# A four-layer graph network on one core: layer 2's own rows moved into the tile of the listed columns, the dense bank copied by ScalarE

## The chip, the core and the metric

The kernel runs on one core of a Trainium2 chip. The metric is device time in microseconds (us) of one execution. Its instructions go to five engines that run side by side, each in its own order: TensorE (matrix products, "PE" in the profile; "PEld" is its weight loads), VectorE (DVE), ScalarE (ACT), GpSimd (POOL) and SyncE (SP), which here only issues DMA transfers. "SPq" marks an issue of a DMA on SyncE's queue. The order on each engine is set when the program is built, by a planner that works with its own estimates of durations; it is not the order of the lines.

## The reference, cut to what matters

Four graph layers over 2708 nodes with 512 features, each of the form `x = x + layer(relu(layernorm(x)), adj)`. The change is in layer 2, a two-step graph convolution, and in the indices that layer 3 shares with it:

```python
def _L2_gnn_ref(x, adj, W1, b1, W3, b3, Wf, bf):
    h = jax.nn.relu(adj @ (x @ W1) + b1)
    h = jax.nn.relu(adj @ (h @ W3) + b3)
    return jnp.tanh(h @ Wf + bf)

def _L3_gnn_ref(input_features, adj, W, b):
    A = (adj != 0).astype(input_features.dtype)
    hidden = input_features @ W + b
    deg = jnp.sum(A, axis=0)
    return A @ hidden / deg[:, None]

h = jnp.maximum(_layernorm(x, axis=-1), 0.0)
x = x + _L2_gnn_ref(h, adj, L2_gnn_W1, L2_gnn_b1, L2_gnn_W3, L2_gnn_b3, L2_gnn_Wf, L2_gnn_bf)
```

`adj` is sparse, and the denser towards the first nodes, with a full diagonal.

## The kernel before

The 2708 rows are worked on in 22 row tiles of 128 (the last, tile 21, has 20 rows). For a row tile `m` the product `adj @ g` has three parts.

- **Dense part**: the first `WHOLE[m]` column tiles (6 for the first tiles, 3 or 4 later) are multiplied in full. Each piece of the matrix (`raw`, up to three column tiles, loaded on SP at L1013) is split into a high, a low and a combined part (ScalarE L1068, VectorE L1069 and L1070), and so is `g`. The products (L1081) collect in two banks of TensorE's accumulator memory: `agg` (called `main` in the function) and `aggs` (`mixed`).
- **Listed part**: of the columns behind, only those with a nonzero are taken. Their numbers were found in layer 0 and stand in `idx_g`, in up to `CHUNKS[m]` chunks of 128 (10 for tile 1, then 9, 8, 7 and on down to 5). The listed columns of the matrix stand in DRAM (`listed[m]`, `lst` in the profile) and are loaded by `load_listed` (SP, L1023) into a tile `ac`, of which there are two buffers. The matching rows of `g` are gathered from DRAM by GpSimd (L1030), one indirect DMA for a chunk, into eight buffers `gg`. The products (L1084) go to `aggs`.
- **Own rows**: for tiles 6 to 20 (`alone(m)`) the diagonal isn't in the lists. The rows of `g` with the tile's own numbers are loaded (SP, L1107) into `u`, multiplied by the diagonal `diag_c` and the bias is added (VectorE, L1108).

`aggregated` then sums the banks: `u = agg * (1 - 2^-12) + bias`, `u = aggs * 2^-12 + u` (both VectorE, L1115; for own rows `bias` is the `u` of L1108). `agg` and `aggs` have two buffers each. `relu_parts` transposes `u` on TensorE (`pt`, L970) and splits it into `v_hi` (ScalarE, L975), `v_lo` and `v_s` (VectorE, L976 and L979), and `project3` multiplies by weights in three parts into the banks `main` and `mixed` (L995).

This happens in two passes over the row tiles. The **first pass** reads `g1d` and writes `g2d` (the products by W3). It also marks the nonzeros for layer 3: ScalarE writes the signs of `ac` and `raw` to `nz` (L1048), stored at L1100. The **second pass** reads `g2d`, and behind the first projection (`main<-wa`, by Wf) a chain runs for each tile: `sum_banks` writes `z` (ScalarE L956, VectorE L957), the bias is added (L1391), tanh (ScalarE L1392, with a load of its table), the residual is added (L1400), layernorm follows (L189 to L199, with another table load), and after a second transpose the second projection (`main<-wb`) gives layer 3's `hidden`. It is stored to `hid` (L1408) and, from tile 3 on, to `hidr` (L1411). The tile `z` carries the name `u` too, so the sums of the banks and `z` share two buffers of that name, which they take in turn. Layer 3 then gathers rows of `hidr` with a second set of indices, `idx_h`, which is `idx_g` less 384 (L1382, in program order behind `aggregated`, for tiles 4 to 20); tile 21 uses `idx_g` and `hid`.

The pool `ap` holds `raw` (three buffers), `ac` (two), `nz` (three) and the split parts; the pool `wp` holds `u`, `v_*` and `go` (two buffers each). Layer 3 uses the name `ac` for its masks (L1305).

The lines of the step around the change:

```python
u = wp.tile([P, D], FP, name="u")
if alone(m):
    nc.sync.dma_start(out=u, in_=gd[span(m)])
    nc.vector.scalar_tensor_tensor(
        u, u, diag_c[:, m : m + 1], bias, op0=ALU.mult, op1=ALU.add
    )
    bias = u
main, mixed = aggregate(m, parts, shifted, gd, marked)
```

Of the kernel before, what the change touches and what calls it, by code (L numbers as in the profile page):

```python
# [9 lines left out]
FP = mybir.dt.float32  # L10
# [34 lines left out]
def kernel(  # L45
# [36 lines left out]
    NB = (N + BLK - 1) // BLK  # L82
    UNIT = 4
    assert N % UNIT == 0
    NCH = 8 * ((max(CHUNKS) + 7) // 8)
    NCA = max(CHUNKS)
    NCL = max(CHUNKS[LEAD:])

    def rows(t):
        return min(P, N - t * P)  # L90
# [60 lines left out]
    flag = const.tile([P, 1], I32, name="flag")  # L151


    idx_g = const.tile([P, NT, NCH], U32, name="idx_g")

    rdeg = const.tile([P, NT], FP, name="rdeg")
    diag_c, self_w = (const.tile([P, NT], FP, name=name) for name in ("diag_c", "self_w"))
# [81 lines left out]
    with tc.tile_pool(name="l0_slab", bufs=2) as slabs, tc.tile_pool(  # L239
# [177 lines left out]
        def search(m):  # L417

            first = dense_of(m) * P
            num = N - first  # L420
            ranks = ranks_of.pop(m)

            end = wp.tile([P, 1], FP, name="end")
            nc.vector.tensor_scalar_add(end, ranks[:, num - 1 : num], 1.0)
            nc.vector.tensor_copy(ranks[:, num : num + 1], end)
            want = wp.tile([P, NCH], FP, name="want")
            nc.vector.tensor_scalar(want, places, end, None, op0=ALU.min)
            for c0 in range(0, CHUNKS[m], 8):
                c = slice(c0, c0 + 8)
                at = wp.tile([P, 8], U32, name="found")  # L430
                nc.vector.max_index(at, want[:, c], ranks)
                nc.vector.tensor_scalar(
                    idx_g[:, m, c],
                    at,
                    float(N - first),
                    float(first),
                    op0=ALU.min,
                    op1=ALU.add,
                )
                node = wp.tile([P, 8], FP, name="node")  # L440
                nc.vector.tensor_scalar(
                    node,
                    at,
                    float(N - 1 - first),
                    float(N // UNIT),
                    op0=ALU.min,
                    op1=ALU.mult,
                )
                nc.vector.tensor_scalar_add(
                    idx_a[:, m, c], node, float((first * N + m * P) // UNIT)  # L450
                )
            nc.vector.tensor_scalar(
                bad[:, BAD_MANY + m : BAD_MANY + m + 1],
                end,
                float(CHUNKS[m] * P + 1),
                None,
                op0=ALU.is_gt,
            )
# [189 lines left out]
        def gather_rows(m):  # L648

            gs = []  # L650
            for c in range(CHUNKS[m]):
                g = hp.tile([P, D], FP, name=f"h{DENSE + gather_slot[0] % NGG}")
                gather_slot[0] += 1
                nc.gpsimd.indirect_dma_start(  # L654
                    out=g,
                    out_offset=None,
                    in_=h0d[:, :],
                    in_offset=bass.IndirectOffsetOnAxis(ap=idx_g[:, m, c : c + 1], axis=0),
                )
                gs.append(g)  # L660
            gathers[m] = gathers[m], gs
# [280 lines left out]
    order_2 = order_m[:1] + order_m[HEAD:] + order_m[1:HEAD]  # L942
    x3_last = dram.tile([P, D], FP, name="x3_last")

    idx_h = gp.tile([P, NT, NCA], U32, name="idx_h")
    NMARK = DENSE + NCA
    gather_slot = [0]

# [70 lines left out]
        return raw[:k, : len(ts), :n], k  # L1019

    def load_listed(m):
        ac = ap.tile([P, NCA, P], FP, name="ac")[:, : CHUNKS[m], : rows(m)]
        nc.sync.dma_start(out=ac, in_=listed[m])  # L1023
        return ac

    def gather(m, gd, gs=None, index=idx_g):

        gs = gs or [gathered() for _ in range(CHUNKS[m])]
        for c in range(CHUNKS[m]):
            nc.gpsimd.indirect_dma_start(  # L1030
                out=gs[c],
                out_offset=None,
                in_=gd[:, :],
                in_offset=bass.IndirectOffsetOnAxis(ap=index[:, m, c : c + 1], axis=0),
            )
        return gs

    def aggregate(m, parts, shifted, gd, marked):


        n = rows(m)
        whole, num = dense_of(m), CHUNKS[m]
        if marked:
            nz = ap.tile([P, NMARK, P], U8, name="nz", bufs=3)

            def mark(i, a):
                k, ts = a.shape[:2]
                nc.scalar.activation(nz[:k, i : i + ts, :n], a, AF.Sign)  # L1048
        main = ps_a.tile([P, D], FP, name="agg") if dense_of(m) else None
        mixed = ps_a.tile([P, D], FP, name="aggs")  # L1050
        chunks = []
        if num:
            ac = load_listed(m)
            chunks = [(ac[:, c, :], g) for c, g in enumerate(gather(m, gd))]
            if marked:
                mark(whole, ac)
        for ts in ([t for t in ts if t < whole] for ts in dense):
            if not ts:
                continue
            gs = [parts(t) for t in ts]  # L1060
            raw, k = load_piece(m, ts)
            hi, lo, s = (
                ap.tile([P, PIECE, P], FR, name=f"a_{part}") for part in ("hi", "lo", "s")
            )
            d = (slice(0, k), slice(0, len(ts)), slice(0, n))
            if marked:
                mark(ts[0], raw)
            nc.scalar.activation(hi[d], raw, AF.Copy, scale=UP)  # L1068
            nc.vector.tensor_tensor(lo[d], raw, hi[d].bitcast(FP), ALU.subtract)  # L1069
            nc.vector.scalar_tensor_tensor(  # L1070
                s[d], lo[d].bitcast(FP), SHIFT, hi[d].bitcast(FP), op0=ALU.mult, op1=ALU.add
            )
            for i, t in enumerate(ts):
                ghi, glo, gs_ = gs[i]
                first, last = t == 0, t == whole - 1
                for acc, a, b, st, sp in (
                    (main, hi, ghi, first, False),
                    (main, lo, glo, False, last),
                    (mixed, s, gs_, first, False),
                ):  # L1080
                    nc.tensor.matmul(acc[:n], a[:k, i, :n], b[:k], start=st, stop=sp)  # L1081
        if chunks:
            for c, (a, g) in enumerate(chunks):
                nc.tensor.matmul(  # L1084
                    mixed[:n],
                    a,
                    g,
                    start=(c == 0 and not dense_of(m)),
                    stop=(c == len(chunks) - 1),
                )  # L1090
        else:
            for ts in others:
                gs = [shifted(t) for t in ts]
                raw, k = load_piece(m, ts)
                for i, t in enumerate(ts):
                    nc.tensor.matmul(  # L1096
                        mixed[:n], raw[:, i, :], gs[i][:k], start=False, stop=(t == NT - 1)
                    )
        if marked:
            nc.sync.dma_start(out=nonzero[m], in_=nz[:, : whole + num, :n])  # L1100
        return main, mixed

    def aggregated(m, parts, shifted, gd, bias, marked=False):
        n = rows(m)
        u = wp.tile([P, D], FP, name="u")
        if alone(m):
            nc.sync.dma_start(out=u, in_=gd[span(m)])  # L1107
            nc.vector.scalar_tensor_tensor(  # L1108
                u, u, diag_c[:, m : m + 1], bias, op0=ALU.mult, op1=ALU.add
            )  # L1110
            bias = u
        main, mixed = aggregate(m, parts, shifted, gd, marked)
        if dense_of(m):
            for bank, scale in ((main, 1.0 - EPS12), (mixed, EPS12)):
                nc.vector.scalar_tensor_tensor(  # L1115
                    u[:n], bank[:n], scale, bias[:n], op0=ALU.mult, op1=ALU.add
                )
                bias = u
        else:
            nc.vector.scalar_tensor_tensor(  # L1120
                u[:n], mixed[:n], EPS12, bias[:n], op0=ALU.mult, op1=ALU.add
            )
        return relu_parts(u, n)
# [138 lines left out]
    def gather_h(m):  # L1262
# [1 line left out]
        whole, num = dense_of(m), CHUNKS[m]  # L1264
        nz = marks[m] = ap.tile([P, NMARK, P], U8, name="nz", bufs=3)
        nc.sync.dma_start(out=nz[:, : whole + num, : rows(m)], in_=nonzero[m])
        gd, index = (hidr, idx_h) if whole else (hid, idx_g)
        listed_h[m] = gather(m, gd, [next(places_h) for _ in range(num)], index)

    def bank_h(m):  # L1270
        if m not in banks:
# [30 lines left out]
    def listed_products(m):  # L1302
        n = rows(m)
        whole, num = dense_of(m), CHUNKS[m]
        mask = ap.tile([P, NCA, P], FR, name="ac")[:, :num, :n]  # L1305
        nc.scalar.copy(mask, marks[m][:, whole : whole + num, :n])
        for c, g in enumerate(listed_h.pop(m)):
            high = part_room()
# [67 lines left out]
    for m in order_2:  # L1376
# [3 lines left out]
            w = split_w(wsetb, wr, "wb")  # L1380
        if dense_of(m) and m not in FULL:
            nc.vector.tensor_scalar_add(  # L1382
                idx_h[:, m, : CHUNKS[m]], idx_g[:, m, : CHUNKS[m]], float(-HEAD * P)
            )
        if m == order_2[-1]:
            for k in order_3[:FIRST]:
# [498 lines left out]
```

## Time and profile before

| what | value |
|---|---|
| three runs, median (lowest to highest) | 1461.38 us (1460.47 to 1461.90) |
| the profiled execution | 1461.3 us |
| its span | 1459.5 us |
| mean granted TensorE clock | 0.929 of full |
| busy: TensorE, VectorE, ScalarE, GpSimd | 1240.7, 954.0, 675.8, 660.6 us |

The page's second part shows the span in 40 equal slices of 36.5 us; each digit is a busy share in tenths, and PEclk is the clock granted to TensorE in tenths:

```profile
PE   4898897889787559989899989899988888967997
DVE  4677996897998568743344356356655666656776
ACT  5865465576344446522222223244443444435563
PEclk9989998989898869999999999999999999978999
```

Layer 2's sums of the banks (L1115) start between 597.5 and 1284.2 us: the first pass stores its last g2d at 908.9 (L1192), the first gather of the second pass starts at 912.1, and the loads of own rows go out from 703.5 to 884.5 and from 986.1 to 1246.0 (L1107). Layer 3 follows. A group in the page's list of groups reads: line, engine, operation, tile written <- tiles read, number of instructions, then busy time and mean duration, then the idle time of the engine just before them with what ended it:

```profile
L1084 PE MATMUL aggs<-gg,ac 128*128 128x512 f32 (+1 forms) x520 | 237.0, 598 | 5.2 <-DMA gg<-g1d,idx_g 5.2
L1108 DVE SCALAR_TENSOR_TENSOR u<-u,diag_c,bias 128x512 f32<-128x512 f32 x30 | 22.6, 752 | 60.5 <-DMA u<-g1d 46.9
```

The first line is the listed products of both passes: two instructions for a chunk, 598 ns each (they overlap). The second is the step of the own rows, 15 tiles in each pass: 752 ns each, and VectorE stood 60.5 us before them in all, 46.9 of it for the first pass's loads. In the lists of waits a line reads: engine, tile and line that waited <- what it waited for: us in total, times, longest. In the lists of instructions: start, duration, engine, line, operation, and in brackets the idle time of the engine before it.

### The profile page before, as it was taken

The numbers are of one execution on the slowest core, as the hardware profiler recorded it, in microseconds if no ns is written. First come the engines' busy times: TensorE is split into PE (matmuls) and PEld (weight loads), VectorE is DVE, ScalarE is ACT, GpSimd is POOL, SyncE is SP. The second block draws the span as 40 slices with busy tenths as digits, with TensorE's granted clock in tenths as the row PEclk, the third lists the DMA queues.
The fourth block names the chain that finished last, engine by engine and source line by source line (L and its number), as shares of the span: only waits on it lengthen the run. The fifth ranks groups of instructions, "written<-read, shape, count | busy, mean of one in ns | idle before, by whom it ended". The sixth has DMA issues, their size and how long they took to land. (4 is left out here: it accounts for less than half of the span.)

```text
span 1459.5 us, 15175 instructions
## 1 busy us (share of the span) xinstructions
PE 1240.7 (85%) x4223; PEld 725.9 (50%) x4223; DVE 954.0 (65%) x2043; ACT 675.8 (46%) x1056; POOL 660.6 (45%) x674
## 2 busy tenths in 40 slices
PE   4898897889787559989899989899988888967997
PEld 2333333334333146746455556466645555545775
DVE  4677996897998568743344356356655666656776
ACT  5865465576344446522222223244443444435563
POOL 1245567656662431055545441444524232355773
PEclk9989998989898869999999999999999999978999
DMA  9988997999886488367868876856746455558895
GB/s 350 339 253 281 330 297 241 315 291 308 260 304 218 130 290 281 112 213 256 261 210 260 272 245 211 268 189 211 216 140 194 144 162 161 172 177 304 278 300 164
DMA packets 187750, 350.68 MB, mean 240 GB/s; under 512 B 22818, under 2 KB 96496, under 8 KB 183925
## 3 DMA queue, kind: packets, MB, share of 16 engines
q1 hardware_dynamic: 140057, 202.48, 42.2%
q0 software_dynamic: 46032, 145.05, 31.5%
q10 hardware_dynamic: 1568, 2.10, 0.4%
q8 instruction: 35, 0.57, 0.2%
q14 instruction: 58, 0.48, 0.1%
HBM read 285.96 MB, written 63.58 MB: 239 GB/s over the span
## 5 line engine op out<-in xcount | busy, mean ns | idle before, releaser
L1030 POOL DMA_INDIRECT gg<-g2d,idx_g x130 | 133.8, 1029 | 244.4 <-PE aggs L1084 200.0
L1084 PE MATMUL aggs<-gg,ac 128*128 128x512 f32 (+1 forms) x520 | 237.0, 598 | 5.2 <-DMA gg<-g1d,idx_g 5.2
L1030 POOL DMA_INDIRECT gg<-g1d,idx_g x130 | 132.5, 1020 | 170.7 <-PE aggs L1084 100.4
L636 POOL DMA_INDIRECT ac<-in_adj_t_dram,idx_a x130 | 131.7, 1013 | 117.6 <-DMA lst<-ac 39.8
L1084 PEld LDWEIGHTS aggs<-gg,ac 128*128 128x128 f32 (+1 forms) x520 | 97.9, 191 | 106.3 <-issue 93.1
L864 PE MATMUL acc<-h,inc 128*128 128x512 f32 (+1 forms) x276 | 139.0, 649 | 9.9 <-DVE inc L704 5.7
L654 POOL DMA_INDIRECT h<-h0d,idx_g x111 | 109.0, 982 | 57.5 <-PE acc L864 28.5
L171 PE MATMUL yacc<-wvo,hT 128*128 128x512 f32 (+1 forms) x176 | 100.2, 708 | 28.9 <-ACT hT L206 24.7
L975 ACT ACTIVATE v_hi<-pt 128x512 fp32r<-128x512 f32 (+1 forms) x88 | 48.6, 578 | 143.1 <-PE pt L970 137.4
L1081 PE MATMUL agg<-ghi,a_hi 128*128 128x512 f32 x180 | 86.5, 481 | 23.9 <-DVE u L1115 20.6
L864 PE MATMUL acc<-h,incl 128*128 128x512 f32 (+1 forms) x222 | 101.1, 598 | 0.3 <-DVE incl L704 0.3
L976 DVE SCALAR_TENSOR_TENSOR v_lo<-pt,v_hi 128x512 fp32r<-128x512 f32 (+1 forms) x88 | 56.8, 666 | 65.6 <-ACT v_hi L975 65.6
L864 PEld LDWEIGHTS acc<-h,inc 128*128 128x128 f32 (+1 forms) x276 | 54.2, 206 | 80.9 <-issue 60.1
L1030 POOL DMA_INDIRECT gg<-hidr,idx_h x62 | 68.2, 1101 | 35.5 <-PE aggs L1281 13.3
L1081 PE MATMUL agg<-glo,a_lo 128*128 128x512 f32 x180 | 78.9, 438 | 3.8 <-ACT glo L220 3.8
L1081 PE MATMUL aggs<-gs,a_s 128*128 128x512 f32 x180 | 74.1, 426 | 3.9 <-DVE a_s L1070 2.3
L171 PEld LDWEIGHTS yacc<-wvo,hT 128*128 128x128 f32 (+1 forms) x176 | 36.4, 219 | 72.3 <-issue 39.3
L571 ACT ACTIVATE sgn<-ar 128x2708 bf16<-128x2708 f32 (+1 forms) x22 | 54.0, 2455 | 36.5 <-DMA ar<-in_adj_dram 36.5
L864 PEld LDWEIGHTS acc<-h,incl 128*128 128x128 f32 (+1 forms) x222 | 41.0, 190 | 49.9 <-issue 45.3
L616 DVE MAX8 top<-ar 128x8 f32<-128x2708 f32 (+1 forms) x22 | 65.4, 2973 | 0.0
L618 DVE FIND_INDEX8 at_top<-top,ar 128x8 uint32<-128x2708 f32 (+1 forms) x22 | 65.4, 2971 | 0.0
L1108 DVE SCALAR_TENSOR_TENSOR u<-u,diag_c,bias 128x512 f32<-128x512 f32 x30 | 22.6, 752 | 60.5 <-DMA u<-g1d 46.9
(347 smaller groups left out, 2767.7 us busy)
## 6 DMA issues: line engine op xcount, KB each, us to landing
ar<-in_adj_dram SPq DMA_DIRECT2D x27, 1354.0 KB
raw<-in_adj_t_dram SPq DMA_DIRECT2D x92, 192.0 KB
slot<-x SPq DMA_DIRECT2D x41, 256.0 KB
at<-in_adj_t_dram SPq DMA_DIRECT2D x26, 256.0 KB
h<-in_x_dram SPq DMA_DIRECT2D x21, 256.0 KB
h0d<-h POOLq DMA_DIRECT2D x21, 256.0 KB, 7.0
xt<-in_x_dram SPq DMA_DIRECT2D x21, 256.0 KB
x<-xt SPq DMA_DIRECT2D x21, 256.0 KB
```

Of the source, the lines that this page charges most:

```text
L171: nc.tensor.matmul(acc[:n], hT[:, c, :n], w[:, c, :], start=(c == 0), stop=(c == NCD - 1))
L571: nc.scalar.activation(sgn[:n], ar[:n], AF.Sign, accum_out=sum_sgn[:n])
L616: nc.vector.max(top[:n], ar[:n])
L618: nc.vector.max_index(at_top[:n], top[:n], ar[:n])
L636: nc.gpsimd.indirect_dma_start(out=ac[:, c, :n], out_offset=None, in_=adj_units, in_offset=bass.IndirectOffsetOnAxis(ap=idx_a[:, m, c0 + c ...
L654: nc.gpsimd.indirect_dma_start(out=g, out_offset=None, in_=h0d[:, :], in_offset=bass.IndirectOffsetOnAxis(ap=idx_g[:, m, c : c + 1], axis=0),)
L864: nc.tensor.matmul(acc[:n], a, g, start=(i == 0), stop=(i == len(pairs) - 1))
L975: nc.scalar.activation(hi[d], pt[d], AF.Relu, scale=UP)
L976: nc.vector.scalar_tensor_tensor(lo[d], pt[d], 0.0, hi[d].bitcast(FP), op0=ALU.max, op1=ALU.subtract)
L1030: nc.gpsimd.indirect_dma_start(out=gs[c], out_offset=None, in_=gd[:, :], in_offset=bass.IndirectOffsetOnAxis(ap=index[:, m, c : c + 1], ax ...
L1081: nc.tensor.matmul(acc[:n], a[:k, i, :n], b[:k], start=st, stop=sp)
L1084: nc.tensor.matmul(mixed[:n], a, g, start=(c == 0 and not dense_of(m)), stop=(c == len(chunks) - 1),)
```

## The change

Three edits go together.

The own rows get a place in the tile of the listed columns: `ac` has 11 chunks of 128 instead of 10, and the last four (512 numbers a row) hold the own rows, which is free for tiles 6 to 20 since these list at most 7 chunks. They are loaded and multiplied inside `aggregate`, right behind the load of the listed columns. `u` is written first by the sum of the banks.

The sum of the dense bank is split: ScalarE copies `agg` times 1 - 2^-12 to `u`, VectorE adds the bias (for tiles 6 to 20 the own rows' part of the `ac` tile), and the other bank is added as before.

`idx_h` is gone: 384 is taken off `idx_g` in place, and `idx_g` loses the row of tile 0, which lists nothing.

```diff
+    assert all(CHUNKS[m] + NCD <= max(CHUNKS) + 1 for m in range(DENSE, NFULL))
...
-    idx_g = const.tile([P, NT, NCH], U32, name="idx_g")
+    idx_g = const.tile([P, NT - 1, NCH], U32, name="idx_g")
+
+    def index_g(m):
+
+        return idx_g[:, m - 1, :]
...
-    idx_h = gp.tile([P, NT, NCA], U32, name="idx_h")
...
     def load_listed(m):
-        ac = ap.tile([P, NCA, P], FP, name="ac")[:, : CHUNKS[m], : rows(m)]
+        both = ap.tile([P, NCA + 1, P], FP, name="ac")
+        ac = both[:, : CHUNKS[m], : rows(m)]
         nc.sync.dma_start(out=ac, in_=listed[m])
-        return ac
+        return ac, both[:, -NCD:, :].rearrange("p c k -> p (c k)")
...
         if num:
-            ac = load_listed(m)
+            ac, spare = load_listed(m)
+            if alone(m):
+                nc.sync.dma_start(out=spare, in_=gd[span(m)])
+                nc.vector.scalar_tensor_tensor(
+                    spare, spare, diag_c[:, m : m + 1], bias, op0=ALU.mult, op1=ALU.add
+                )
+                bias = spare
             chunks = [(ac[:, c, :], g) for c, g in enumerate(gather(m, gd))]
...
-        return main, mixed
+        return main, mixed, bias
...
         u = wp.tile([P, D], FP, name="u")
-        if alone(m):
-            nc.sync.dma_start(out=u, in_=gd[span(m)])
+        main, mixed, bias = aggregate(m, parts, shifted, gd, marked, bias)
+        if dense_of(m):
+            nc.scalar.activation(u[:n], main[:n], AF.Copy, scale=1.0 - EPS12)
+            nc.vector.tensor_add(u[:n], u[:n], bias[:n])
             nc.vector.scalar_tensor_tensor(
-                u, u, diag_c[:, m : m + 1], bias, op0=ALU.mult, op1=ALU.add
-            )
-            bias = u
-        main, mixed = aggregate(m, parts, shifted, gd, marked)
-        if dense_of(m):
-            for bank, scale in ((main, 1.0 - EPS12), (mixed, EPS12)):
-                nc.vector.scalar_tensor_tensor(
-                    u[:n], bank[:n], scale, bias[:n], op0=ALU.mult, op1=ALU.add
-                )
-                bias = u
+                u[:n], mixed[:n], EPS12, u[:n], op0=ALU.mult, op1=ALU.add
+            )
...
-        gd, index = (hidr, idx_h) if whole else (hid, idx_g)
-        listed_h[m] = gather(m, gd, [next(places_h) for _ in range(num)], index)
+        listed_h[m] = gather(
+            m, hidr if whole else hid, [next(places_h) for _ in range(num)]
+        )
...
             nc.vector.tensor_scalar_add(
-                idx_h[:, m, : CHUNKS[m]], idx_g[:, m, : CHUNKS[m]], float(-HEAD * P)
+                index_g(m)[:, : CHUNKS[m]], index_g(m)[:, : CHUNKS[m]], float(-HEAD * P)
             )
```

The other places that read `idx_g` (the search that fills it, the gathers of layers 0, 2 and 3) go through `index_g(m)`, and layer 3's masks take the new size of `ac`.

More of the change, by code (lines that the diff above doesn't have):

```diff
@@ L432, in search @@
                 nc.vector.tensor_scalar(
-                    idx_g[:, m, c],
+                    index_g(m)[:, c],
                     at,
@@ L657, in gather_rows @@
                     in_=h0d[:, :],
-                    in_offset=bass.IndirectOffsetOnAxis(ap=idx_g[:, m, c : c + 1], axis=0),
+                    in_offset=bass.IndirectOffsetOnAxis(
+                        ap=index_g(m)[:, c : c + 1], axis=0
+                    ),
                 )
@@ L1021, in load_listed, with gather @@
     def load_listed(m):
-        ac = ap.tile([P, NCA, P], FP, name="ac")[:, : CHUNKS[m], : rows(m)]
+        both = ap.tile([P, NCA + 1, P], FP, name="ac")
+        ac = both[:, : CHUNKS[m], : rows(m)]
         nc.sync.dma_start(out=ac, in_=listed[m])
-        return ac
-    def gather(m, gd, gs=None, index=idx_g):
+        return ac, both[:, -NCD:, :].rearrange("p c k -> p (c k)")
+    def gather(m, gd, gs=None):
         gs = gs or [gathered() for _ in range(CHUNKS[m])]
@@ L1033, in gather, with aggregate @@
                 in_=gd[:, :],
-                in_offset=bass.IndirectOffsetOnAxis(ap=index[:, m, c : c + 1], axis=0),
+                in_offset=bass.IndirectOffsetOnAxis(
+                    ap=index_g(m)[:, c : c + 1], axis=0
+                ),
             )
         return gs
-    def aggregate(m, parts, shifted, gd, marked):
+    def aggregate(m, parts, shifted, gd, marked, bias):
         n = rows(m)
@@ L1304, in listed_products @@
         whole, num = dense_of(m), CHUNKS[m]
-        mask = ap.tile([P, NCA, P], FR, name="ac")[:, :num, :n]
+        mask = ap.tile([P, NCA + 1, P], FR, name="ac")[:, :num, :n]
         nc.scalar.copy(mask, marks[m][:, whole : whole + num, :n])
```

## The prediction

> **What bounds it.** I read the page's busy shares first (TensorE 85%, VectorE 65%, ScalarE 46%), then the table by stage, then who waited for whom on TensorE in each stage, then the order of instructions through one row tile. Layer 2's second pass begins at 912 us, and its last own rows are loaded at 1246. The first table is of all instructions, the second of the dense products (L1081) alone; the columns are the stretch, its length, and the busy time (instructions) of TensorE, its weight loads and, in the first, VectorE, ScalarE and GpSimd, then granted clock, DMA share and GB/s.
>
> ```profile
> 986.00:1104.00 118.00, 111.81 (x410) 69.80 (x410) 75.03 (x143) 51.01 (x77) 50.57 (x50) 0.97 0.63 194
> 1104.00:1250.00 146.00, 124.98 (x444) 82.55 (x443) 91.72 (x166) 61.76 (x88) 45.93 (x43) 0.93 0.54 161
> ...
> 986.00:1104.00 118.00, 23.94 (x83) 15.66 (x83) 0.97 0.63 194
> 1104.00:1250.00 146.00, 31.30 (x90) 20.88 (x90) 0.93 0.54 161
> ```
>
> Until 1104 TensorE is nearly full. From 1104 it idles 21.0 us of 146, and the list of its waits there has just two lines:
>
> ```profile
> PE agg L1081 <- DVE u L1115: 20.6, 8, 3.8
> PE aggs L1081 <- DVE u L1115: 0.4, 2, 0.2
> ```
>
> So eight times the dense product of a tile waits for `u` to empty the bank of the tile two before it (`agg`, `aggs` have two buffers each). One of the eight, by engine:
>
> ```profile
> 1211.54 0.32 SPq L1408 DMA_DIRECT2D hid<-go  x1
> 1212.43 0.41 SPq L1107 DMA_DIRECT2D u<-g2d  x1
> 1213.72 0.32 SPq L1023 DMA_DIRECT2D ac<-lst  x1
> ...
> 1212.01 0.60 ACT L956 ACTIVATE u<-main 128x512 f32<-128x512 f32 x1 [2.28 <-PE main L995]
> ...
> 1212.94 0.69 DVE L957 SCALAR_TENSOR_TENSOR u<-mixed,u 128x512 f32<-128x512 f32 x1 [0.64 <-PE mixed L995]
> 1213.66 0.69 DVE L1391 TENSOR_TENSOR u<-u,bias 128x512 f32<-128x512 f32 x1
> 1215.30 0.75 DVE L1108 SCALAR_TENSOR_TENSOR u<-u,diag_c,bias 128x512 f32<-128x512 f32 x1 [0.94 <-DMA u<-g2d]
> 1215.96 0.69 DVE L1400 TENSOR_TENSOR slot<-slot,u 128x512 f32<-128x512 f32 x1
> 1216.57 0.69 DVE L1115 SCALAR_TENSOR_TENSOR u<-agg,u 128x512 f32<-128x512 f32 x1
> ...
> 1212.67 1.02 PE L1084 MATMUL aggs<-gg,ac 128*128 128x512 f32 x2
> 1217.31 0.79 PE L1081 MATMUL agg<-ghi,a_hi 128*128 128x512 f32 x1 [3.62 <-DVE u L1115]
> ```
>
> The name `u` has two buffers, which the sums of this tile and `z` of the one before (L956) take in turn. The load of own rows starts 0.4 us after `z` is first written, though the transposes freed both buffers at 1207; I read from it that a `u` gets its buffer only once the preceding `z` has its own. The row takes 2.87 us to the start of L1108, VectorE stands 0.94 us, then L1108, L1400 and L1115 go one after another, and TensorE starts 0.05 us after the last. The chain that ended last runs through this load (its by-line summary has it at 1.6%).
>
> **The change, part by part.** The sum is made against the profiled execution: 1461.3 us, of which 1459.5 is span. The three other runs have a median of 1461.38 (1460.47 to 1461.90), so it stands for them.
>
> *The wait goes.* The dense bank no longer waits for the rows: ScalarE copies it. `u` may be written after `z`'s copy (1212.61); a copy of this form takes 0.60 (L956), so `agg` is free at 1213.2, and TensorE is there at 1213.69. Gain 21.0. The other end: the copy queued behind the table load (1.28), the gap before tanh (0.5) and tanh (0.63) ends at 1215.6, 1.9 us late here, 0.2 to 1.9 elsewhere, some 9 us in all. I take the early place, since all that the copy needs is there then.
>
> *The slower products after a gap.* A dense product takes 31.30/90 = 348 ns in this stage and 23.94/83 = 288 before 1104, at clocks of 0.93 and 0.97: 60 ns x 90 = 5.4 us. With two thirds of the gaps gone I take 3.4; the ends are 0 and 5.4. The Trainium skill (TensorE: Matmul & The Clock Gate, rules for authors) allows idle gaps up to about 3 us before the clock falls; the rows show starts 0.43 us apart already behind a gap of 2.75. By the page three gaps alone would count and this term would be some 2 us.
>
> *The listed tile is held longer.* This is the new wait. Own rows and listed columns share a tile with two buffers, and it comes free only when `u` has added the rows, not, as now, when TensorE has finished the listed products (L1023 follows the last of them by 0.03). With `u` allowed only after `z`, the add comes behind L957 and L1391: 1212.94 + 3 x 0.72 = 1215.1. Then the load of the listed columns for the tile after next: issued in 0.1, landed in 2.9 to 3.3 (the row's 2.87, a little more for 320 KB than 256): 1218.2, 5.5 us after TensorE begins the rest of the listed products. What TensorE can do meanwhile is that rest (0.9 to 3.4 us by tile, 0.43 for each L1084) plus nine to twelve dense products (2.5 to 3.3): for the eight tiles 5.2, 5.2, 3.9, 6.0, 3.5, 5.2, 3.5 and 5.2. What 5.5 leaves is 0.3, 0.3, 1.6, 0, 2.0, 0.3, 2.0 and 0.3: 6.8 us. From 986 to 1104, where seven chunks give 7 to 8.5 us of cover, one tile with 4.2 adds 1.3. I take 8.1. The low end is 0: transposes and products of `u` could fill it. The high end, a load that lands as the one issued at 884.00 did (6.4 us, to ScalarE's mark at 890.4), is a gate of 8.8: 33 + 9 = 42. On SP the waiting load holds back the loads of `raw` (L1013) and the next stores, but the next of these went out at 1221.79, long after.
>
> *ScalarE and VectorE.* 42 copies x 0.597 = 25.1 us more on ScalarE, which idles 84 of 146 us here. On the path the copy pushes tanh's table load back by 0.6, of which 0.5 was waiting for L1391: 0.1 x 8, about 1 us. The page ScalarE: Activation LUTs (Rules for kernel authors) speaks against it: plain multiplying belongs on VectorE. The rows say otherwise for this bank: 597 ns on ScalarE, 684 on VectorE (L1115). By the page the move would cost ScalarE time for nothing. VectorE keeps its number of instructions: one sum from a bank at 684 becomes an add at 691 (L1391's), 7 ns x 42 = 0.3. The multiply by the diagonal stays at 752.
>
> *The indices.* `idx_h` was written by 17 instructions of 159 ns at 506 us, where VectorE had stood 9.6 us. Written in place, each waits until that tile's gathers have landed, so they move into the second pass: 2.7 us, behind them whatever VectorE holds next (`v_lo` above all, for which the projections wait). Landing is 3.9 us at the median and 6.7 at most. TensorE didn't wait for gathers in this pass, so they land well ahead: I take half of the 2.7, 1.4. Ends: 0, and 17 x 2.8 = 48 if each write came up to the median and met the slowest gather.
>
> *The first pass.* There the row load already stands right behind the listed load, and both are late:
>
> ```profile
> 884.00 0.38 SPq L1023 DMA_DIRECT2D ac<-lst  x1
> 884.49 0.37 SPq L1107 DMA_DIRECT2D u<-g1d  x1
> ...
> DVE u L1108 <- DMA u<-g1d: 46.9, 15, 5.9
> ACT nz L1048 <- DMA ac<-lst: 65.9, 19, 6.6
> ```
>
> The rows leave when they did, so the 46.9 us remain; `u` alone uses its name there, so its add precedes the end of the listed products and the tile isn't held. ScalarE's copy can queue behind a mark (65.9/19 = 3.5 us), which 4.3 us of listed products cover; at the longest, 6.6, the cover is 2.3 short, 15 tiles, 35 us. The gain is at most 7.9, the five small TensorE gaps before transposes (1.77, 1.55, 1.07, 2.61, 0.89); the sixth, 7.25, followed a late read of g2d on ScalarE. Taken: 0. Issues keep their number: the row load moves behind the listed load on SP, past hid's and hidr's stores, 0.4 us. Layer 3 gathers as before.
>
> Sum: -21.0 - 3.4 + 8.1 + 1.0 + 0.3 + 1.4 = -13.6: **1447.7, say 1448 us**.
>
> **Rivals.** (a) *Slower: the held tile is the bound.* For it: the 5.5 us gate is just above the cover of seven tiles, and a first-pass load took twice my 3.1. Against it: DMA is half idle here (0.54). At a gate of 7 the waits are 18.3 + 2.8 = 21.1, which with the other terms (2.7) eats the 24.4 won: it decides from 1.5 us of lateness. At 8: 26.3 + 6 = 32, so 11 slower: 1472.
> (b) *Slower: VectorE stands at the index writes.* For: in-order, and 17 of them. Against: gathers end early. It decides at 13.6/17 = 0.8 us on the path per tile; at 1.5, 1473.
> (c) *No change:* `z` and `u` are still transposed as a pair (x8), and TensorE, earlier at that point by 2.6 us, waits there for `z`. For: TensorE begins the pair at 1205.35, 1.1 us after `z` is ready. Against: with the three `u` steps out of `z`'s way (0.94 + 0.66 + two of 0.6) `z` comes 2.8 us earlier too. 1461.
> (d) *All of it:* the held tile is covered and the small gaps of the first pass go: -21.0 - 5.4 - 7.9 + 2.7 = -31.6, 1430. For: spare projections. Against: every cover must hold.
>
> **How the numbers follow.** 0.54 for the forecast (its own range 1438 to 1457), (d) 0.12, (c) 0.06, (a) 0.17, (b) 0.08, and 0.03 for an order of instructions on the engines that is worse elsewhere: it isn't the order of the lines and changes with such an edit. Faster by over 0.2% (2.9 us, about what a measurement tells from no change) 0.66, within it 0.06, slower 0.28. The range 1434 to 1472 leaves out half of (d) and about half of (a) and (b).
>
> **What would show it.** Right: in the second pass no wait of `agg` for `u`, ScalarE's copy of `agg` within 1 us of `z`'s, TensorE's idle from 1104 halved, listed loads issued after the add of own rows. (a) shows as TensorE waiting for `ac` from DMA; (b) as VectorE waiting at L1382 for gathers; (c) as transposes waiting for L199. I am wrong if `u` gets a buffer before `z` (then the tile isn't held and it is (d)), or if the first pass, taken as 0, moves by over 5 us.

## The result: slower by 2.6%

The changed kernel takes 1497.38 us (median of 4 runs, 1493.24 to 1502.23), the kernel before 1460.93 us beside it (4 runs, 1451.47 to 1461.90). The ratio is 1.026, with an interval of 1.022 to 1.030. The forecast was 1448 us; what happened is the rival that had VectorE standing at the index writes. Here and below medians are of all runs, while a ratio with an interval leaves out runs more than 1.5% above the fastest of their kernel.

The profiled execution of the changed kernel has a span of 1494.9 us, against 1459.5. Cut at four marks of both traces, the span reads:

| stretch | before | after |
|---|---|---|
| start to the first store of g2d (layers 0 and 1, start of layer 2) | 644.1 | 638.8 |
| first pass, to the first gather of the second pass | 268.0 | 268.0 |
| second pass, to the last store of hid | 406.4 | 443.7 |
| to the end (layer 3) | 141.0 | 144.4 |

So the second pass loses 37.3 us, more than the whole difference of 35.4. The start gains 5.3, and the end loses 3.4.

The page of the changed kernel, first the slices of the span (36.5 us before, 37.4 here):

```profile
PE   4898878978868489899799988787789988966997
PEclk9989999999889689999899999988999999978998
```

From the 25th to the 30th slice (897 to 1121 us) TensorE's row has 8, 7, 8, 7, 7, 8; the row of the kernel before has 9, 8, 9, 9, 9, 8 in these slices. Who waited for whom on TensorE in most of the second pass (907 to 1283 us; engine, tile and line <- what it waited for: us, times, longest):

```profile
PE main L1001 <- DVE v_lo L982: 18.8, 10, 5.5
PE pt L976 <- ACT u L204: 15.4, 5, 6.5
PE mixed L1001 <- DVE v_s L985: 8.5, 2, 4.8
PE aggs L1099 <- DMA ac<-lst: 5.0, 7, 0.9
...
PE agg L1096 <- ACT u L1123: 2.3, 7, 0.3
```

The wait of `agg` for `u` is down from 20.6 us to 2.3. In its place stand waits for things that VectorE makes: `v_lo`, `v_s`, and the `u` of layernorm, whose `shift` is VectorE's. Over the whole second pass TensorE idles 75.9 us where it idled 46.4, and is busy 367.8 where it was 360.0: the waits for `v_lo`, `v_s` and `u` of layernorm are 40.7 us more, that of `agg` is 18.3 less, and the listed tile `ac` adds 5.0. VectorE's own list for the same stretch begins with the reason:

```profile
DVE idx_g L1392 <- DMA gg<-g2d,idx_g: 72.3, 16, 8.2
```

Sixteen of the seventeen index writes (L1392, the old L1382 made to write in place) stood for a gather, 72.3 us in all and up to 8.2 at once. One of them on the engines, for tile 10:

```profile
1071.89 0.95 POOL L1037 DMA_INDIRECT gg<-g2d,idx_g  x1 [0.30 <-issue]
...
1070.70 0.16 DVE L199 RECIPROCAL rstd<-rstd 128x1 f32<-128x1 f32 x1 [0.36 <-ACT rstd L198]
1079.11 0.17 DVE L1392 TENSOR_SCALAR idx_g<-idx_g 128x6 uint32<-128x6 uint32 x1 [8.25 <-DMA gg<-g2d,idx_g]
1079.19 0.21 DVE L201 TENSOR_SCALAR shift<-mv,rstd 128x1 f32<-128x1 f32 x1
...
1079.49 0.81 ACT L204 ACTIVATE u<-slot,shift,rstd 128x512 f32<-128x512 f32 x1 [8.83 <-DVE shift L201]
...
1080.36 1.97 PE L976 MATMUL pt<-ident,u 128*128 128x128 f32 x8 [6.53 <-ACT u L204]
```

The write takes 384 off the six columns of indices that this tile's six gathers read. They are issued from 1065.50 to 1071.89; the last lands 7.2 us later, and the write starts at 1079.11. They go out this late because they wait for room: ahead of the first GpSimd stood 8.48 us for TensorE's listed products to use up a buffer `gg`, and 227.3 us in 49 such waits from 907 to 1283 us. VectorE had been done with `rstd` at 1070.86. `shift`, which needs nothing but `rstd`, stands behind the write in VectorE's order, and so do ScalarE's normalisation and TensorE's transposes: 8.25, 8.83 and 6.53 us of idle time, one behind the other, with one instruction of 0.17 at their head. In a later tile:

```profile
1178.21 0.60 ACT L962 ACTIVATE u<-main 128x512 f32<-128x512 f32 x1 [2.50 <-PE main L1001]
1178.70 0.59 ACT L1123 ACTIVATE u<-agg 128x512 f32<-128x512 f32 x1
...
1179.73 0.68 DVE L1124 TENSOR_TENSOR u<-u,ac 128x512 f32<-128x512 f32 x1
...
1180.48 0.32 SPq L1030 DMA_DIRECT2D ac<-lst  x1
...
1189.92 0.17 DVE L1392 TENSOR_SCALAR idx_g<-idx_g 128x5 uint32<-128x5 uint32 x1 [3.43 <-DMA gg<-g2d,idx_g]
1190.00 1.28 DVE L982 SCALAR_TENSOR_TENSOR v_lo<-pt,v_hi 128x512 fp32r<-128x512 f32 x2
...
1190.74 1.20 PE L1001 MATMUL main<-wb,v_lo 128*128 128x512 f32 x4 [0.38 <-DVE v_lo L982]
```

Here the write holds `v_lo` for 3.43 us, but TensorE still had the products by `v_hi` to do and loses 0.38. The rest of the lines are as forecast: ScalarE's copy of `agg` follows `z`'s by 0.5 us, and the listed columns are loaded when the own rows have been added.

### The profile page after: what moved, and what is told of

The parts are those of the page before. It is cut to its first block, busy times and chain, and to the rows that moved or that the text cites. A ratio compares the mean times of both kernels' runs of the same rounds, so it can differ in the third digit from the quotient of the medians.

```text
span 1494.9 us, 15277 instructions
## 1 busy us (share of the span) xinstructions
PE 1244.3 (83%) x4223; PEld 720.6 (48%) x4223; DVE 953.1 (64%) x2043; ACT 696.0 (47%) x1098; POOL 656.0 (44%) x674
## 5 line engine op out<-in xcount | busy, mean ns | idle before, releaser
L1037 POOL DMA_INDIRECT gg<-g2d,idx_g x130 | 129.9, 1000 | 275.7 <-PE aggs L1099 227.3
L1099 PE MATMUL aggs<-gg,ac 128*128 128x512 f32 (+1 forms) x520 | 233.2, 594 | 10.5 <-DMA gg<-g1d,idx_g 5.4
L176 PE MATMUL yacc<-wvo,hT 128*128 128x512 f32 (+1 forms) x176 | 96.9, 687 | 28.3 <-ACT hT L211 28.3
L1037 POOL DMA_INDIRECT gg<-hidr,idx_g x62 | 70.1, 1130 | 35.5 <-issue 13.4
L1096 PE MATMUL agg<-glo,a_lo 128*128 128x512 f32 x180 | 75.5, 419 | 3.9 <-ACT glo L225 3.9
L1096 PE MATMUL aggs<-gs,a_s 128*128 128x512 f32 x180 | 70.4, 410 | 4.2 <-DVE u L1125 2.6
L976 PE MATMUL pt<-ident,u 128*128 128x128 f32 (+1 forms) x264 | 40.9, 290 | 39.7 <-ACT u L204 22.0
L1001 PE MATMUL main<-wb,v_lo 128*128 128x512 f32 (+1 forms) x176 | 52.2, 421 | 18.8 <-DVE v_lo L982 18.8
L871 PEld LDWEIGHTS acc<-h,incl 128*128 128x128 f32 (+1 forms) x222 | 41.1, 191 | 50.3 <-issue 46.6
```

Of the source, the lines that this page charges most:

```text
L176: nc.tensor.matmul(acc[:n], hT[:, c, :n], w[:, c, :], start=(c == 0), stop=(c == NCD - 1))
L871: nc.tensor.matmul(acc[:n], a, g, start=(i == 0), stop=(i == len(pairs) - 1))
L976: nc.tensor.transpose(pt[:, c, :n], v[:n, c * P : (c + 1) * P], ident[:n, :n])
L1001: nc.tensor.matmul(acc[:n], a[:, c, :n], b[:, c, :], start=first and c == 0, stop=last and c == NCD - 1,)
L1037: nc.gpsimd.indirect_dma_start(out=gs[c], out_offset=None, in_=gd[:, :], in_offset=bass.IndirectOffsetOnAxis(ap=index_g(m)[:, c : c + 1], ...
L1099: nc.tensor.matmul(mixed[:n], a, g, start=(c == 0 and not dense_of(m)), stop=(c == len(chunks) - 1),)
```

## The experiments

The runs were made on four chips, and each ratio is against runs of the kernel before on the same chip: 1534.52 us for the x runs, 1552.65 for the y runs, 1457.20 for the z runs and 1541.71 for the w runs. Where an expectation names times, they are on the scale of the first chip (1460.93).

### One part at a time: the indices apart, the indices alone

x1 is the changed kernel with layer 3's indices in a small tile of their own, written from `idx_g` as the kernel before does. To find room for it, `idx_g` is packed.

```diff
+    idx_h = gp.tile([P, NFULL - 4, NIH], U32, name="idx_h")
...
-                index_g(m)[:, : CHUNKS[m]], index_g(m)[:, : CHUNKS[m]], float(-HEAD * P)
+                idx_h[:, m - 4, : CHUNKS[m]], index_g(m)[:, : CHUNKS[m]], float(-HEAD * P)
```

> The changed kernel with layer 3's indices again in a tile of their own (17 tiles of up to 7 columns; idx_g is packed to make room), so no instruction writes over indices that gathers still read. Theory 'index writes' (VectorE stands 72.3 us in the second pass at L1392 until a tile's gathers have landed, and the projections wait for the v_lo behind it): the loss goes, no wait on gathers on VectorE; with the eight waits of agg for u gone too, 1440 to 1455. Theory 'held tile' (the listed columns' tile comes free too late): stays at 1480 or above, TensorE still waits for ac. Theory 'order' (the planner's order came out worse, whatever the cause): anything, with VectorE's wait gone and TensorE's idle time in the second pass at other places, still above 1475.

x2 is the kernel before with that one edit: its indices written in place, nothing else changed.

```diff
-    idx_h = gp.tile([P, NT, NCA], U32, name="idx_h")
...
-        gd, index = (hidr, idx_h) if whole else (hid, idx_g)
+        gd, index = (hidr if whole else hid), idx_g
...
-                idx_h[:, m, : CHUNKS[m]], idx_g[:, m, : CHUNKS[m]], float(-HEAD * P)
+                idx_g[:, m, : CHUNKS[m]], idx_g[:, m, : CHUNKS[m]], float(-HEAD * P)
```

> The kernel before with one edit: 384 is taken off idx_g in place, no idx_h. Theory 'index writes': VectorE waits at these writes as in the changed kernel (40 to 80 us in all), 1480 to 1510. Theory 'held tile': no change, 1461 within 3. Theory 'order': a few us either way without a large wait on VectorE for gathers.

Measured: x1 1524.30 us, 0.993 of the kernel before by the medians, without an interval (three of its four runs took 1523.66 to 1526.61 us, one 1499.92, so this is rough); x2 1568.04 us, ratio 1.0213 (1.0144 to 1.0282). The second pass takes 407.5 us in x1 and 456.8 in x2. VectorE's longest wait in x2's second pass, and then two of TensorE's there:

```profile
DVE idx_g L1381 <- DMA gg<-g2d,idx_g: 42.0, 12, 7.6
```

```profile
PE agg L1080 <- DVE u L1114: 21.6, 8, 3.7
...
PE main L994 <- DVE v_lo L975: 10.7, 3, 4.0
```

The in-place write alone makes the kernel before slower by about as much as the whole change does, and the eight old waits for `u` are still there beside the new ones. Without it the change is no longer slower. TensorE's list in x1's second pass has no wait for `v_lo`, and has the held tile:

```profile
PE pt L979 <- ACT u L205: 10.4, 3, 6.1
...
PE aggs L1100 <- DMA ac<-lst: 5.5, 7, 1.0
```

So the rival with the held tile is real and small: seven waits of up to 1.0 us.

### Is it the place of the own rows or ScalarE's copy?

x3 is x1 with the dense bank summed by VectorE again, the bias or own rows added in the same instruction.

```diff
-            nc.scalar.activation(u[:n], main[:n], AF.Copy, scale=1.0 - EPS12)
-            nc.vector.tensor_add(u[:n], u[:n], bias[:n])
+            nc.vector.scalar_tensor_tensor(
+                u[:n], main[:n], 1.0 - EPS12, bias[:n], op0=ALU.mult, op1=ALU.add
+            )
```

> As the run with the indices apart, but VectorE sums the dense bank as before (no copy by ScalarE), so only the own rows' place differs from the kernel before. If the own rows' load alone was what the eight waits of agg for u stood behind, this gains as much as the run with the copy (within 5 us of it); if the copy by ScalarE is what frees the bank, agg still waits for u on VectorE in the second pass, 1450 to 1461. Theory 'held tile': above 1475.

Measured: 1522.43 us, ratio 0.9929 (0.9890 to 0.9967), within what x1's four runs can tell of x1; the second pass takes 414.0 us, against 407.5 in x1. The wait of `agg` for `u` is down to 0.9 us here too, in TensorE's list of the second pass (two lines of it):

```profile
PE pt L979 <- ACT u L205: 16.0, 7, 6.1
...
PE agg L1097 <- DVE u L1124: 0.9, 6, 0.2
```

The transposes wait more than in x1 instead (16.0 against 10.4 us). The early load of the own rows is what removed the eight waits. The copy on ScalarE isn't needed for that. Whether the copy without the early load would do it as well was not run.

### The same write in place, but later

x4 is the changed kernel with the write in place, made to depend on a cell that is written behind the tile's residual sum. By then all of that tile's gathers have been used. `idx_g` is packed as in x1.

```diff
-        if dense_of(m) and m not in FULL:
-            nc.vector.tensor_scalar_add(
-                index_g(m)[:, : CHUNKS[m]], index_g(m)[:, : CHUNKS[m]], float(-HEAD * P)
-            )
...
         nc.vector.tensor_add(xt[:n], xt[:n], z[:n])
+        if dense_of(m) and m not in FULL:
+            off = wp.tile([P, 1], FP, name="off", bufs=1)
+            nc.vector.tensor_scalar(
+                off, xt[:, :1], 0.0, float(-HEAD * P), op0=ALU.mult, op1=ALU.add
+            )
+            nc.vector.tensor_scalar(
+                index_g(m)[:, : CHUNKS[m]],
+                index_g(m)[:, : CHUNKS[m]],
+                off,
+                None,
+                op0=ALU.add,
+            )
```

> The changed kernel with the writes in place kept, but each made to depend on the residual sum of its tile (its -384 comes from a cell written behind L1410), by when the gathers have long landed; idx_g packed to make room for that cell. Theory 'index writes': what costs is the wait and not the write, so it lands within 6 us of the run with the indices apart, 1442 to 1460, and VectorE stands under 5 us for gathers. Theory 'held tile' or 'order': 1475 or above.

Measured: 1512.76 us, ratio 0.9881 (0.9812 to 0.9949), the second pass 407.1 us, and no wait of VectorE for a gather at the write. Writing in place costs nothing that shows here; writing when VectorE comes to it before the gathers have landed is what costs the 2.6%. The packing isn't the reason: x2 and z3 below, without it, differ in nothing but the late write, and have 1.0213 and 0.9893 (on two chips).

### Which of the seventeen

The y runs first repeat both kernels. y1 is the kernel before, y2 the changed kernel.

> The kernel before, profiled on the same chip as its neighbours here, since the chip of the first four runs was slower than the first one in the stages that no edit touches. Every theory: the second pass near 406 us if that chip's slowness lies in the earlier layers, and the eight waits of agg for u near 21 us.

> The changed kernel on this chip. Theory 'index writes': the same loss as on the first chip, 1.020 to 1.032 of before, and VectorE stands 60 to 80 us at L1392. If the loss belonged to one chip, 1.00 to 1.01.

Measured: y1 1555.58 us with a second pass of 429.9; y2 1575.04 us, ratio 1.0149 (1.0096 to 1.0203), second pass 459.9, 65.9 us of VectorE's time at the writes. The eight waits of `agg` are in y1 too (20.2 us). But y1's second pass isn't near the 406 us that I expected, so this chip is slower there as well, and the loss in y2 falls short of the expected 1.020, though it is of the same kind.

y3 is the changed kernel with tiles 4 to 11 written in place and tiles 12 to 20 apart.

```diff
+    idx_h = gp.tile([P, NFULL - 12, NIH], U32, name="idx_h")
+
+    def index_h(m):
+
+        return idx_h[:, m - 12, :] if 12 <= m < NFULL else index_g(m)
```

> The changed kernel with the indices of tiles 4 to 11 taken down in place (8 writes) and those of tiles 12 to 20 in a tile apart (9 writes). Theory 'index writes': the loss goes by the writes that wait, so between the changed kernel and the run with all apart, 0.998 to 1.018 of before, and the second pass is slow only while tiles 4 to 11 are worked on. Theory 'order': no such split, the loss stays whole (above 1.02) or is gone (below 0.996).

Measured: 1575.04 us (1551.03 to 1583.66), ratio 1.0093 (1.0035 to 1.0152), second pass 453.5 us. The median is that of y2, and the ratios' intervals overlap, so the times don't show how the loss divides; the traces do. TensorE's longest waits there, first in the stretch of the early tiles (976 to 1197 us), then in that of the later ones (1197 to 1330):

```profile
PE main L1009 <- DVE v_lo L990: 16.4, 4, 6.1
PE pt L984 <- ACT u L205: 9.5, 2, 6.6
PE mixed L1009 <- DVE v_s L993: 8.5, 2, 4.3
```

```profile
PE aggs L1105 <- DMA ac<-lst: 3.7, 6, 0.8
PE aggs L1102 <- DVE u L1131: 2.8, 6, 0.7
```

VectorE stands 46.6 us at eight writes. The waits for `v_lo` and `v_s` are all in the early tiles, and of the 30.0 us that the second pass of y2 is longer than y1's, y3 keeps 23.6. By these traces the eight writes of the early tiles, whose gathers are more (six and seven chunks) and come later against VectorE, make most of the loss.

y4 is x4 without ScalarE's copy (x3's edit).

> The late write in place with VectorE's two sums as before (no copy by ScalarE). The run with VectorE's sums gained as much as the one with the copy, so if the copy adds nothing, this is within 5 us of the late write with the copy: 0.985 to 0.995 of before. If the copy is worth something once VectorE no longer waits, 0.993 to 1.00.

Measured: 1529.76 us, ratio 0.9854 (0.9823 to 0.9884). Against y2 on the same chip, the late write is worth 45.3 us, with the copy off as well.

### A version that beats both, and a surprise

The z runs time x4 and y4 in five rounds, and the kernel before with a late write in place (x2's edit, the write moved as in x4) as a control, which should change nothing.

> The late write with ScalarE's copy once more, on one chip with its neighbour without the copy. If the copy adds nothing beside the own rows' place, both have the same ratio within 0.4%, 0.983 to 0.990 of before. If the copy gains (it frees the dense bank 3 us earlier), this is the faster by 5 us or more; if it costs (one more step ahead of tanh's table load, and bank sums that VectorE has to do anyway), the slower by 5 us or more.

> The late write with VectorE's two sums, as in the earlier run: 0.982 to 0.990 of before, the best version so far if the copy adds nothing or costs.

> The kernel before with one edit: the write in place, made late by the cell behind L1400. Theory 'index writes': written in place the loss was 2.1% with VectorE waiting 42 us for gathers; written late there is no such wait, 0.997 to 1.004 of before. If the 34 more VectorE instructions in the second pass cost by themselves, 1.005 or more.

| | us | ratio to before | second pass |
|---|---|---|---|
| z1, own rows early, copy on ScalarE, late write | 1436.97 | 0.9857 (0.9833 to 0.9881) | 391.9 |
| z2, the same with both sums on VectorE | 1442.45 | 0.9897 (0.9867 to 0.9928) | 390.4 |
| z3, before with the late write alone | 1441.91 | 0.9893 (0.9865 to 0.9922) | 395.5 |

z1 has the lowest ratio of the three and beats both kernels. But the control gained 1.1% where I expected nothing, so z1 has only 0.4% over z3, and z2 nothing, with intervals that overlap: what the own rows' place is worth beside a late write isn't told by these rounds. By the traces z2's second pass is 5.1 us shorter than z3's, and its first pass 7.1 longer (269.7 against 262.6). TensorE's waits in the second pass of z3, z2 and z1, one fence each:

```profile
PE agg L1080 <- DVE off L1398: 20.0, 8, 3.3
PE pt L969 <- ACT u L199: 7.5, 3, 4.6
```

```profile
PE pt L977 <- ACT u L205: 16.2, 8, 6.1
```

```profile
PE pt L977 <- ACT u L205: 9.0, 2, 6.1
...
PE aggs L1100 <- DMA ac<-lst: 4.8, 7, 0.9
```

z3 still has the eight waits of `agg` (put down to VectorE's cell `off` now). z2 has lost them and shows eight waits of the transposes for layernorm's `u`, 8.7 us more than z3: my rival of no change, in part. z1 has two such waits, and the held tile.

What did the control gain? Its difference to the kernel before is that the seventeen writes are gone from the start of layer 2, which the changed kernel does as well. There, in the kernel before and then in the changed one (two fences):

```profile
506.47 1.35 DVE L1382 TENSOR_SCALAR idx_h<-idx_g 128x7 uint32<-128x7 uint32 x17 [9.62 <-DMA bias<-in_L_gnn_b_dram]
507.73 1.28 DVE L212 TENSOR_TENSOR wb<-wr,wb 128x512 fp32r<-128x512 f32 x2
...
507.99 5.49 POOL L1146 DMA_INDIRECT slot<-y,idx  x1 [0.30 <-issue]
513.78 0.95 POOL L1146 DMA_INDIRECT slot<-y,idx  x1 [0.30 <-issue]
```

```profile
502.05 1.29 DVE L217 TENSOR_TENSOR wb<-wr,wb 128x512 fp32r<-128x512 f32 x2 [4.73 <-ACT wb L215]
...
508.28 0.98 POOL L1155 DMA_INDIRECT slot<-y,idx  x1 [0.30 <-issue]
509.56 0.95 POOL L1155 DMA_INDIRECT slot<-y,idx  x1 [0.30 <-issue]
```

The writes stood in VectorE's order ahead of the splitting of the weights `wb`, and held it back by 5.7 us. So the sums of `wb` ran beside the gathers of layer 2's first rows, and one gather took 5.49 us instead of 0.98; what lengthened it isn't shown (see the last section). Both kernels pass the last count of signs before this (ScalarE) at 485.6 and 485.5 us, and come to the same `v_hi` early in layer 2 at 532.2 and 527.0: 5.1 of the 5.3 us that the changed kernel gains in the first stretch are won here. On two other chips the same stretch differs by less: 45.7 and 44.9 us in x1 and x3, which have the writes there, against 44.7 and 44.6 in x2 and x4, and 45.4 in y1 against 43.9 and 43.5 in y2 and y4.

Three more runs asked whether this is a matter of the writes or of the tile `idx_h`, and whether z3 was one chip's luck. w1 is the kernel before. w2 is z3 again. w3 keeps `idx_h` and only moves its writes behind the residual sums.

```diff
...
+            nc.vector.tensor_scalar(
+                idx_h[:, m, : CHUNKS[m]], idx_g[:, m, : CHUNKS[m]], off, None, op0=ALU.add
+            )
```

> The kernel before, unchanged, profiled on the chip of the two runs beside it, so that their stages can be laid side by side. If the moved index writes are what the kernel before loses (theory A), its stretch from the last transposes of layer 1 to the first product of layer 2 is some 5 us longer than theirs, VectorE standing some 9 us ahead of seventeen index writes there. If the 1.1% was one chip's luck (theory B), the stages are alike within 3 us each.

> The kernel before with the late write in place, a second time. Theory A: ratio 0.986 to 0.993 again, some 5 us of it before the first store of g2d. Theory B: 0.997 to 1.003.

> The kernel before with its own idx_h kept and only its seventeen writes moved from the start of layer 2 to behind each tile's residual sum. Theory A (the writes at the start stand in VectorE's queue ahead of what layer 2 begins with): as w2, 0.986 to 0.993, no stand of VectorE before layer 2. Theory C (it is not the writes but the tile idx_h itself, whose room frees late, that costs): 0.997 to 1.003, while w2 stays at 0.99.

Measured: w2 1534.97 us, ratio 0.9945 (0.9912 to 0.9978); w3 1532.24 us, ratio 0.9943 (0.9906 to 0.9980); w1 one run of 1529.87. The two ways gain the same, so it is the moved writes and not the tile's room. The gain is half of z3's, under what was expected of the writes, and its place isn't shown on this chip: from those signs to that `v_hi` w1 takes 45.3 us, w2 45.4 and w3 44.9, against 46.6 and 39.6 in the first trace of the kernel before and in z3. The long gather is 2.92 us in w1, and the longest of the first eight 1.52 in w2 and 1.48 in w3. That part of the expectation failed: a stand of 6.2 us at the writes is in w1, but the sums of `wb` start 0.76 us behind ScalarE's first part of `wb` there and 0.65 in w2, so it held them back by some 0.1 us (6.56 us lie between the two in the first trace). The second passes take 428.0, 425.4 and 418.5 us; but the traced run of w1 is 11.8 us below its kernel's median, so single traces can't place a gain of this size. Where the rest of the gain of 0.55 to 1.1% lies stays open.

## Why the prediction was wrong, point by point

**The step that failed is "The indices".** It took half of the 2.7 us, 1.4, from the sentence "TensorE didn't wait for gathers in this pass, so they land well ahead". That asks the wrong engine. TensorE comes to a tile's listed products last, behind the dense ones and the projections; VectorE comes to the write when its order has it, and the order has the write of one tile ahead of `shift` and `v_lo` of the tiles before it. For VectorE the gathers are late by 3.3 to 8.3 us in the eight early tiles and by 1.9 to 4.2 in the later ones: they go out only as TensorE frees the buffers `gg`. For TensorE the same gathers are early: those of tile 10 had landed at 1079.09, and it took them up from 1085.59. TensorE's price in the stretch shown is 18.8 + 8.5 for `v_lo` and `v_s`, and for `pt` 15.4 against 5.5 before: 37.2 us, or 2.2 for each write, where the sum had 1.4 in all. (That this is so near the second pass's loss of 37.3 is chance: the waits of `agg` that went, the new ones for `ac` and 7.8 us more of busy time belong to that account too.) With the writes moved back the kernel is 45.3 us shorter (y4 against y2, and y4 has no copy on ScalarE). The upper end that I had written, 48 us, was near; the rival decided from 0.8 us per tile, and I gave it 0.08. The page Perfetto Trace Analysis of the Trainium skill (Tensor Engine Instruction) says that VectorE takes its instructions in strict order; the line of 1079.11 shows it, with the `shift` that needed only `rstd` standing 8.25 us behind a write it has nothing to do with.

**The wait goes: right.** 20.6 us became 2.3. But the reason given, that ScalarE copies the bank, isn't what it took: in x3 the early own rows do it alone. Without the copy the transposes wait more.

**The slower products after a gap: right in kind, and it moved.** In the later stretch (1110 to 1283) a dense product takes 30.68/108 = 284 ns at a clock of 0.99, where it took 348 at 0.93. In the early stretch (907 to 1110), where the new gaps are, it takes 40.77/126 = 324 ns at 0.91; from 912 to 1104 the kernel before had 43.26/144 = 300 at 0.96.

**The listed tile is held longer: right in kind, too large.** 8.1 was the term, 5.0 was measured (5.5 in x1, 4.8 in z1), in seven waits of at most 0.9 us. The loads go out right behind the add of the own rows, as argued.

**ScalarE and VectorE: right.** The copy takes 0.59 us and follows `z`'s by 0.5. What the copy is worth is small and not settled: the medians of x1 and x3 differ by 1.87 us of 1524 (their second passes by 6.5, 407.5 and 414.0), and z1 and z2 by 0.4% with intervals that overlap, and not in the second pass (391.9 and 390.4 us).

**The first pass: right.** 268.0 us both times; the wait for the own rows is 51.1 us of VectorE's, 46.9 before, and it costs nothing there.

**What the sum lacked.** It had the writes leaving the start of layer 2 as a row of 17 x 159 ns beside a stand of 9.6 us, and drew nothing from it. The writes themselves stood, with `wb` behind them; the changed kernel gains 5.1 us there by the two first traces, and on the three other chips with traces of both kinds the same stretch differs by less than 2 us.

Without the indices' term the sum was -15.0 us. x3, whose writes stay where they were, has a ratio of 0.9929, which is -10.4 us of 1461, with -4.8 and -16.1 as the ends (x3 lacks the copy): as a sum, the other terms hold within that interval.

## What to carry to other kernels

An instruction that overwrites what a DMA still reads waits for that DMA, and on an engine that works in order everything behind it waits too; ask when *that engine* comes to it, not when the data's users do. A small write that is needed late should be tied to something late: here TensorE waited 37 us behind the same seventeen writes in one place and for none of them in another. And when a wait for data is seen ahead of a trifling instruction, look at what stands behind it before taking the wait for idle time.

## What the runs showed of the hardware

The chips differ by more than the change: the kernel before took 1457.20, 1534.52, 1541.71 and 1552.65 us (medians) on four of them. Against the first trace (644.1, 268.0, 406.4 and 141.0 us), y1 has 704.3, 276.7, 429.9 and 142.8: layers 0 and 1 make most of it, the last layer hardly any. Ratios from different chips agree only roughly too (the changed kernel 1.026 and 1.0149, the late write in the kernel before 0.9893 and 0.9945).

In all five traces that have the seventeen writes at the start of layer 2 one gather beside VectorE's sums of `wb` is long: 5.49 us in the kernel before, 2.63 in x1, 3.00 in x3, 3.07 in y1 and 2.92 in w1. Each of the five ends 0.85 to 0.88 us behind the last of these sums, which is nearly what a gather takes alone (0.95), as if it had stood until they were through. In the eleven other traces the longest of the first eight gathers takes 1.55 us. The sums alone don't do it: in w3 and z3 gathers of 0.99 and 1.11 us ran wholly beside them. The Trainium skill's page SBUF — State Buffer (Who interferes with whom) describes a port pair that VectorE and GpSimd share and that one of them can hold for a whole instruction; but it infers that sums of two tiles leave the making of descriptors alone. The traces show the lengthening and not its cause: no run here tried the sums and the gathers by themselves.
